# A two-layer graph kernel on one Trainium2 core: the turn to attention in another order, and more of the MLP in the last attention pass

## The chip, the core and the metric

The kernel runs on one core of one Trainium2 chip. The time is device time in microseconds (us); the number quoted for a kernel is the median of several executions. One further execution was recorded by the hardware profiler. Engines are named as in the profile: PE is TensorE (PEld its weight loads), DVE is VectorE, ACT is ScalarE, POOL is GpSimd, SP is SyncE, which here only issues DMAs.

## What is computed

The graph has 3327 nodes of 1024 features, and an adjacency matrix of which about 1% is set. The two layers, cut to what matters:

```python
# layer 0
h  = relu(layernorm(x))
s  = quant4(relu(quant4(h) @ quant3(norm(weight)) * deltas))
x  = x + adj @ s * deltas
# layer 1: attention with 8 heads of 64, then an MLP
h  = relu(layernorm(x))
Wh = einsum('nf,hfd->hnd', h, W)
e  = leaky_relu(e_src[:, :, None] + e_dst[:, None, :], 0.2)   # Wh.a1, Wh.a2
att = softmax(where(adj > 0, e, -9e15), axis=-1)
enc = elu(att @ Wh), heads side by side                       # 3327 x 512
out = relu(enc @ W1.T + b1); out = relu(out @ W2.T + b2); out = relu(out @ W3.T + b3)
x   = x + out @ W4.T + b4
```

## The kernel before

**Layer 0.** The nodes are 26 tiles of 128 rows. For each row tile t, PE sums adjacency times support over all 26 column tiles in fp32r, with each adjacency block as a high and a low half (L717). Adjacency pieces `at` of up to 7 blocks are loaded by SP (L186); ACT makes `hi` (L190), DVE makes `lo` (L194) and one mask byte per edge (L195), which POOL stores to `mask_d` (L201). The result is emptied by ACT into `y` (L732, called `emptied` in the code), scaled by DVE (L733, `resumed`), added to `x` (L734), stored by POOL (L735), and normalised on DVE and ACT up to the factor `r` (L738, `lacking`).

**Heads.** y must be transposed for the product with the head weights. For tiles 0 to 24 this is done by DMA (`transposed_by_dma`): ACT splits y into halves of words (L612), SP issues two transposing DMAs (L614; the second is `turned`), and ACT joins the halves to `ht` (L617). For the last tile PE transposes (`transposed_by_tensor`: two batches of four, L632, each copied from PSUM by ACT, L636). `heads` then runs 8 fp32 matmuls, which the trace shows as 16 records (`whm`, L646), empties them on ACT (`wht`, L653, `taken`), and works out the source and destination scores (L660, L661), their exponentials (L666, L686: ACT loads an exp table for them) and the feature rows (L687 to L697), which POOL stores.

**Attention** is 32 passes: 8 heads by 4 sets of destination tiles (7, 6, 7 and 6 of them, `SUBS`). A pass walks through 13 pairs of source tiles in 7 groups (`GROUPS`; six of two pairs, and pair 6 alone). `select` makes the selectors for a group, two groups ahead of their use: for each source tile a comparison `over` of a row of scores, `srow`, with that tile's scores (ACT, L839; pair 6 on DVE, L833), then per pair an AND with the mask (L846) and an XOR (L847) on DVE. `sums` multiplies selectors with features (L866): 7 tiles x 8 matmuls in a group, into 7 PSUM banks. `closing` finishes a pass (L885 to L914) in slices between the next pass's groups.

**The turn** from layer 0 is written out by hand. On PE the order is: last layer-0 tile, whm of tile 24, sums of group 0, first and second transposes of tile 25, sums of group 1, whm of tile 25, sums of group 2. `queue_behind(a, b)` puts a behind b on their engine without a semaphore; `pin` keeps an instruction in program order on its engine; `issue_after` holds a DMA back until another instruction has run. All adjacency masks come back from `mask_d` through SP (L792), as do the score rows (L801) and features (L786). The scores of groups 0 and 1 (8 pieces of `over`) are ordered ahead of `emptied`.

**The end.** In the last pass `first_layer` runs the first MLP layer of the first group of four node tiles between the groups of sums (L1022, ReLU L1030), through one PSUM bank (`m_ps`). After the pass come that group's second and third layer (L1096, ReLU L1106), and then for each pair of tiles seven products that make up the fourth layer (L1164), from sums of blocks of weights (`weight_sums`, L1066) and of activations (`combined`), with the next group's layers in gaps between them. `joined` loads and joins (L1117) the attention output of a group. Buffers: `over` has 2, `sel` 6, `m_ps` 1, `yo` (output rows) 3.

Of the kernel before, what the change touches and what calls it, by code (L numbers as in the profile page):

```python
# [8 lines left out]
F32 = mybir.dt.float32  # L9
BF16 = mybir.dt.bfloat16  # L10
F32R = mybir.dt.float32r
U8 = mybir.dt.uint8
# [10 lines left out]
P = 128  # L23
# [4 lines left out]
F = 1024  # L28
# [38 lines left out]
def two_layer_kernel(  # L67
# [105 lines left out]
    with tc.tile_pool(name="at", bufs=2, reuse_waits="tile") as atp:  # L173
# [419 lines left out]
        with tc.tile_pool(name="wh", bufs=1, reuse_waits="tile") as whp, tc.tile_pool(  # L593
# [10 lines left out]

            def transposed_by_dma(y):


                ht = s2.tile([P, KF, P], F32, name="ht", bufs=1)
                parts = []
                for c in range(FC):  # L610
# [3 lines left out]
                    last = nc.sync.dma_start_transpose(yht, yh.rearrange("p two f -> p (two f)"))  # L614
                    parts.append(yht)
                for c, yht in enumerate(parts):
                    nc.scalar.copy(  # L617
                        halves_of_words(
                            ht[:, c * KF // FC : (c + 1) * KF // FC].rearrange("p k i -> p (k i)")
                        ),  # L620
                        yht.rearrange("p (two k) i -> p two (k i)", two=2),
                    )
                return ht, last
# [130 lines left out]
            of_k, products, *_, taken = heads(*before, own=f_even)  # L754
            queue_behind(products[0], lacking)
            queue_behind(taken, lacking)
            ht, turns, copies = transposed_by_tensor(y)
            last_of_k, *_ = heads(T - 1, ht, r, own=f_even)
# [6 lines left out]
    with tc.tile_pool(name="over", bufs=2, reuse_waits="tile") as overp, tc.tile_pool(  # L765
        name="srow0", bufs=1, reuse_waits="tile"
    ) as srow0, tc.tile_pool(name="sel", bufs=6, reuse_waits="tile") as selp, tc.tile_pool(
        name="srow1", bufs=1, reuse_waits="tile"
    ) as srow1, tc.tile_pool(name="f1", bufs=1, reuse_waits="tile") as f1p, tc.tile_pool(
# [20 lines left out]
        def load_mask(si, js=slice(0, T)):  # L790
            for b, t in enumerate(SUBS[si]):
                ins = nc.sync.dma_start(masks[si][:, b, js], mask_d[t][:, js])  # L792
            return ins
# [3 lines left out]
        def load_src(i):  # L797
            h, si = attends[i]
            nb = len(SUBS[si])
            srows[i] = (srow1 if i % 2 else srow0).tile([P, 7, P], F32, tag="srow", name="srow")[:, :nb]  # L800
            return nc.sync.dma_start(  # L801
                srows[i].rearrange("p b i -> p (b i)"), src_d[si][h].partition_broadcast(P)
            )
# [17 lines left out]
        def select(n):  # L821
            ends = {}
            i, g = steps[n]
            h, si = attends[i]
            nb = len(SUBS[si])
            mask = masks[si].bitcast(U32)
            for pair in GROUPS[g]:
                over = overp.tile([P, 7, 2, P], U8, tag="over", name="over")[:, :nb]
                for q in range(2):
                    j = 2 * pair + q  # L830
                    if pair in BY_VECTOR:
                        pin(
                            nc.vector.tensor_scalar(  # L833
                                over[:, :, q], srows[i], ndst[:, j, h : h + 1], 255.0, ALU.is_gt, ALU.mult
                            )
                        )
                    else:
                        ends["scalar"] = pin(
                            nc.scalar.activation(  # L839
                                over[:, :, q], srows[i], AF.Relu, bias=large_dst[:, j, h : h + 1], scale=BIG  # L840
                            )
                        )
                sel = selp.tile([P, 2, 7, 2, P], U8, tag="sel", name="sel")
# [95 lines left out]
        select(0)  # L939
        ends = select(1)  # L940
        queue_behind(emptied, ends["scalar"])
        queue_behind(resumed, ends["vector"])
        turn = [(of_k[-1], turns[0][0]), (turns[-1][1], last_of_k[0]), (last_of_k[-1], None)]
        closed = None
        first_group = iter(())
        for n, (i, g) in enumerate(steps):
            if n + AHEAD < len(steps):
                select(n + AHEAD)
# [6 lines left out]
            if (i, g) == (len(attends) - 1, 0):  # L955
# [4 lines left out]
                def nodes(name):  # L960
# [8 lines left out]
                rest = large(mlp, "rest", [P, 7 * NP // 4])  # L969
                bb4 = rest[:, :F]  # L970
                bb1, bb2, bb3 = (rest[:, F + 4 * q : F + 4 * q + 4] for q in range(3))
                h1_0 = rest[:, F + 16 : F + 16 + D1 // P * 512].rearrange("p (m c) -> p m c", c=512)
                enct0 = rest[:, 2 * F + 16 : 2 * F + 16 + EMB // P * 512].rearrange(
                    "p (k c) -> p k c", c=512
# [34 lines left out]
                nc.sync.dma_start(bb4, b4.partition_broadcast(P))  # L1009

                def first_layer():

                    for k in range(EMB // P):

                        nc.scalar.copy(
                            halves_of_words(enct0[:, k]), by_feature(enc_x1[0][0], 512)[:, :, k]
                        )
                        yield
                    for m in range(D1 // P):
                        ps = m_ps.tile([P, 512], F32, tag="mps", name="h0_ps")  # L1020
                        for k in range(EMB // P):
                            nc.tensor.matmul(  # L1022
                                ps,
                                w1[:, k, m * P : (m + 1) * P],
                                enct0[:, k],
                                start=(k == 0),
                                stop=(k == EMB // P - 1),
                            )
                            if k == EMB // P - 1:
                                nc.scalar.activation(  # L1030
                                    h1_0[:, m], ps, AF.Relu, bias=bb1[:, m : m + 1]
                                )
                            yield

                first_group = first_layer()
# [14 lines left out]
        w4c = [[w4[:, 2 * k : 2 * k + 2, c * 512 : (c + 1) * 512] for c in range(FC)] for k in range(2)]  # L1050
        t2, t3, t4 = (
            masks[3].rearrange("p b j i -> p (b j i)").bitcast(F32)[:, n * F : (n + 1) * F].rearrange(
                "p (k c) -> p k c", k=2
            )
            for n in range(3)
        )
        t1 = w4c[0][1]

        def weight_sums():
            for d, one, other in (  # L1060
                (t3, w4c[1][1], w4c[0][1]),
                (t1, w4c[0][1], w4c[0][0]),
                (t2, w4c[1][1], t1),
                (t4, w4c[1][0], t2),
            ):
                pin(nc.vector.tensor_tensor(d, one, other, ALU.subtract))  # L1066
                yield

        of_weight = weight_sums()
        next(of_weight)  # L1070
        next(closed)
        next(of_weight)
        next(of_weight)
        for _ in closed:
            pass
        next(of_weight)


    with tc.tile_pool(name="s4", bufs=2, reuse_waits="tile") as s4, tc.tile_pool(
# [3 lines left out]
        enc_x1.append(nodes("nodes1"))  # L1083
# [169 lines left out]
```

## Time and profile before

| What | Value |
|---|---|
| Median of three runs | 2150.71 us (2149.31 to 2151.26) |
| The profiled execution | 2151.75 us |
| Its span in the trace | 2150.0 us |
| Mean granted PE clock | 0.994 |
| Layer 0 ends on PE (last L717) | 905.66 us |
| Sums of group 2 begin | 943.91 us |
| Last sums of attention end | 1872.97 us |
| Third MLP layer begins (L1096) | 1885.29 us |

The span lies inside the profiled execution's own time. Times within the trace count from the span's start. In a profile row, `x` gives the number of instructions, a number in brackets at the end is idle time of the engine just before the row and what ended it, and PEclk is the share of the full clock that PE was granted.

### The profile page before, as it was taken

Reading aid. Unit: us, or ns where it says so; the run is one execution under the profiler, and the core shown is the slowest. Engines: PE = TensorE matmul, PEld = TensorE weight load, DVE = VectorE, ACT = ScalarE, POOL = GpSimd, SP = SyncE. Lnnn points to the kernel's source line nnn. Section 1 sums busy time; section 2 is a strip of 40 time slices with the busy share of each in tenths; the row PEclk is TensorE's granted clock in tenths of the full one; section 3 lists DMA queues with packets and bytes.
Section 4 is the critical chain, followed back from the end, with each engine's and each line's share of the span. In section 5 each row is a group of like instructions: output and inputs, shape, how many; then the busy total and the mean of one; then the engine's idle time right before and its main releaser. Section 6 shows DMA issues by size and latency. Waiting matters only on the chain.

```text
span 2150.0 us, 36618 instructions
## 1 busy us (share of the span) xinstructions
PE 2101.4 (98%) x15099; PEld 1693.6 (79%) x15109; DVE 1406.8 (65%) x2564; ACT 1347.6 (63%) x1752; POOL 155.8 (7%) x243
## 2 busy tenths in 40 slices
PE   5999999999999999989999999999999999999999
PEld 2467777777777777779999999999999999744444
DVE  8845556555655566467777777777777777635446
ACT  6734454445544554668888888888888888542321
POOL 2300000000100000100000000000000000000000
PEclk9999999999999999989999999999999999999999
DMA  6654544455445544771202021120212114453322
GB/s 217 173 167 137 160 153 136 140 168 153 131 142 165 155 134 147 215 264 26 74 17 74 22 53 46 25 73 19 70 25 74 26 30 126 102 126 108 102 94 74
DMA packets 184648, 233.22 MB, mean 108 GB/s; under 512 B 103924, under 2 KB 133060, under 8 KB 184480
## 3 DMA queue, kind: packets, MB, share of 16 engines
q1 hardware_dynamic: 169692, 178.40, 27.8%
q0 software_dynamic: 14720, 52.41, 7.9%
q8 instruction: 118, 1.93, 0.4%
q14 instruction: 50, 0.41, 0.1%
q10 hardware_dynamic: 68, 0.06, 0.0%
HBM read 141.21 MB, written 66.02 MB: 96 GB/s over the span
## 4 chain that ended last, share of the span: by engine, by line
PE 56%; DVE 1%; ACT 0%; issue 0%; DVEq 0%; ACTq 0%
PE acc L866 43%; PE o L1164 7%; PE h_ps L1096 5%; PE h_ps L1022 0%; PE whm L646 0%; ACT enct L1117 0%; DVE su L885 0%; DVE mask L1066 0%; DVE over L833 0%; DVE su L890 0%; DVE prod L660 0%; DVE ft L687 0%; DVE ft L692 0%; DVE weights L1066 0%; DVE stats L146 0%
## 5 line engine op out<-in xcount | busy, mean ns | idle before, releaser
L866 PEld LDWEIGHTS <-sel 128*128 128x128 fp8e4 x10816 | 935.1, 98 | 9.8 <-issue 8.3
L839 ACT ACTIVATE over<-srow,large_dst 128x896 uint8<-128x896 f32 (+1 forms) x768 | 685.9, 975 | 31.7 <-DVE sel L846 31.7
L866 PE MATMUL acc<-f_even,sel 128*128 128x195 bf16 x5408 | 470.8, 249 | 5.6 <-ACT wht L653 5.6
L866 PE MATMUL acc<-f_odd,sel 128*128 128x195 bf16 x5408 | 467.2, 248 | 0.0
L717 PE MATMUL mm<-s_int,hi 128*128 128x512 f32 x1352 | 426.3, 396 | 0.0
L717 PE MATMUL mm<-s_int,lo 128*128 128x512 f32 x1352 | 416.8, 390 | 0.0
L846 DVE TENSOR_TENSOR sel<-over,mask 128x448 uint32<-128x448 uint32 (+1 forms) x416 | 244.0, 587 | 210.3 <-ACT over L839 123.1
L717 PEld LDWEIGHTS mm<-s_int,hi 128*128 128x128 f32 x1352 | 254.0, 188 | 62.4 <-issue 11.5
L717 PEld LDWEIGHTS mm<-s_int,lo 128*128 128x128 f32 x1352 | 253.8, 188 | 52.7
L847 DVE TENSOR_TENSOR sel<-sel,mask 128x448 uint32<-128x448 uint32 (+1 forms) x416 | 246.0, 591 | 14.2
L190 ACT CAST hi<-at 128x896 fp32r<-128x896 f32 x104 | 92.4, 889 | 153.7 <-PE mm L717 73.4
L646 PE MATMUL whm<-whead,ht 128*128 128x512 f32 x416 | 182.7, 592 | 0.0
L195 DVE TENSOR_SCALAR mk<-at 128x896 uint8<-128x896 f32 (+1 forms) x104 | 59.3, 590 | 173.5 <-DMA at<-in_adj_t 173.5
L194 DVE TENSOR_TENSOR lo<-at,hi 128x896 fp32r<-128x896 f32 x104 | 106.2, 1021 | 68.3 <-ACT hi L190 68.1
L646 PEld LDWEIGHTS whm<-whead,ht 128*128 128x128 f32 x416 | 78.9, 190 | 89.0 <-issue 86.8
L885 DVE TENSOR_REDUCE su<-acc 128x130 f32<-128x390 f32 x208 | 115.8, 556 | 12.2 <-PE acc L866 12.2
L914 POOL DMA_DIRECT2D enc_d<-eh x64 | 57.5, 903 | 856.8 <-ACT eh L912 827.7
L899 ACT ACTIVATE ht<-su,rs 128x64 f32<-128x64 f32 x208 | 53.1, 335 | 104.8 <-DVE rs L895 104.8
L1106 ACT ACTIVATE h<-h_ps,rest 128x512 f32<-128x512 f32 (+1 forms) x54 | 35.3, 655 | 126.3 <-PE h_ps L1096 126.3
L342 PE MATMUL mm<-w_int,xqt 128*128 128x512 bf16 x406 | 93.5, 384 | 7.1 <-DVE w_int L473 4.5
L653 ACT ACTIVATE wht<-whm,lnr 128x512 f32<-128x512 f32 x26 | 17.8, 686 | 121.3 <-PE whm L646 116.4
L617 ACT COPY ht<-yht 128x1024 uint16<-128x1024 uint16 x50 | 67.5, 1355 | 34.0 <-DMA yht<-yh 34.0
(184 smaller groups left out, 1696.0 us busy)
## 6 DMA issues: line engine op xcount, KB each, us to landing
at<-in_adj_t SPq DMA_DIRECT2D x52, 448.0 KB, 4.7
feat_d<-fw POOLq DMA_DIRECT2D x26, 780.0 KB, 6.4
at<-in_adj_t SPq DMA_DIRECT2D x52, 384.0 KB, 4.1
x_d<-xt POOLq DMA_DIRECT2D x26, 512.0 KB, 2.9
nodes<-x_d SPq DMA_DIRECT2D x26, 512.0 KB, 5.5
xt<-in_x SPq DMA_DIRECT2D x25, 512.0 KB, 4.0
out<-yo SPq DMA_DIRECT2D x50, 256.0 KB, 2.2
xs<-in_x SPq DMA_DIRECT2D x24, 512.0 KB, 4.4
```

The costliest lines, as they stand in the source:

```text
L190: ins = nc.scalar.copy(hi, at)
L194: nc.vector.tensor_tensor(lo, at, hi.bitcast(F32), ALU.subtract)
L342: nc.tensor.matmul(mms[t][:, r], xqts[t][:, k, :], w_int[:, k, r], start=(k == 0), stop=(k == KF - 1))
L646: ins = nc.tensor.matmul(whm, ht[:, k, :], whead[:, k, :], start=(k == 0), stop=(k == KF - 1))
L717: nc.tensor.matmul(mm[:, c * 512 : (c + 1) * 512], which[:, q, :], s_int[j][:, c * 512 : (c + 1) * 512], start=(j == 0 and which is hi), s ...
L839: nc.scalar.activation(over[:, :, q], srows[i], AF.Relu, bias=large_dst[:, j, h : h + 1], scale=BIG)
L846: pin(nc.vector.tensor_tensor(up, over.bitcast(U32), of_pair, ALU.bitwise_and))
L847: ends["vector"] = pin(nc.vector.tensor_tensor(dn, up, of_pair, ALU.bitwise_xor))
L866: ins = nc.tensor.matmul(accs[i, b][:, r], chosen[i, pair][:, s, b, q], f[:, j, r], start=(j == 0 and s == 0), stop=(j == T - 1 and s == 1),)
L885: nc.vector.tensor_reduce(su[:, b], accs.pop((i, b)).rearrange("p (q s c) -> p q c s", q=2, s=3), AX.X, ALU.add)
L1096: ins = nc.tensor.matmul(pss[m][:, :cols], wt[:, k, m * P : (m + 1) * P], xt[:, k, :cols], start=(k == 0), stop=(k == k_n - 1),)
L1164: nc.tensor.matmul(ps, st[:, k, q // 2], mv[:, k], start=(k == 0), stop=(k == 1))
```

## The change

Five things are changed.

1. Both halves of mask 0 (14 DMAs) are issued on POOL's queue and without a wait for anything on SP.
2. The pools of the two score rows change places in the order of allocation, so that `srow0` takes another address, and the load of the first row stands on SP ahead of both transposes of tile 24.
3. On ACT, the scores of group 0 stand first, then both joins of tile 24, then `emptied`; the scores of group 1 follow. `copies[0]` (the first PSUM copy of tile 25) is ordered behind `taken` of tile 24, the first exponential of tile 24 (`ratio`, L666) behind the second copy, and the scores of group 2 behind `taken`.
4. `over` is laid out as 2 x (7 x 128) bytes in place of 7 x 2 x 128; the AND reads it through a rearranged view.
5. The end: buffers for a second group are allocated in the last pass, and that group's first loads are issued there. In that pass group 0's joins stand at group 1, the first and second layer's matmuls at groups 2 to 6 (3, 3, 2, 2 and 2 matmuls), and the weight sums and the second group's joins at group 5. After the pass: third layer of group 0, first layer of group 1, then the products. The loads and joins of later groups are issued after the first pair's products.

```diff
-            of_k, products, *_, taken = heads(*before, own=f_even)
+            of_k, products, _, powers, _, taken = heads(*before, own=f_even)
             queue_behind(products[0], lacking)
             queue_behind(taken, lacking)
             ht, turns, copies = transposed_by_tensor(y)
+            queue_behind(copies[0], taken)
+            queue_behind(powers[0], copies[-1])
...
-        name="srow0", bufs=1, reuse_waits="tile"
-    ) as srow0, tc.tile_pool(name="sel", bufs=6, reuse_waits="tile") as selp, tc.tile_pool(
         name="srow1", bufs=1, reuse_waits="tile"
-    ) as srow1, ...
+    ) as srow1, tc.tile_pool(name="srow0", bufs=1, reuse_waits="tile") as srow0, tc.tile_pool(
+        name="sel", bufs=6, reuse_waits="tile"
...
-                over = overp.tile([P, 7, 2, P], U8, tag="over", name="over")[:, :nb]
+                over = overp.tile([P, 2, 7 * P], U8, tag="over", name="over")[:, :, : nb * P]
...
-                                over[:, :, q], srows[i], AF.Relu, bias=large_dst[:, j, h : h + 1], scale=BIG
+                                over[:, q], srows[i], AF.Relu, bias=large_dst[:, j, h : h + 1], scale=BIG
...
+                over = over.bitcast(U32).rearrange("p q (b i) -> p b q i", b=nb)
-                pin(nc.vector.tensor_tensor(up, over.bitcast(U32), of_pair, ALU.bitwise_and))
+                pin(nc.vector.tensor_tensor(up, over, of_pair, ALU.bitwise_and))
...
-        ins = load_mask(0, slice(0, TH))
-        with tc.issue_after(ins.ins):
-            ins = load_src(0)
-        queue_behind(turned, ins)
+        for js in (slice(0, TH), slice(TH, T)):
+            load_mask(0, js, nc.gpsimd)
+        queue_behind(planes[0], load_src(0))
         with tc.issue_after(turned.ins):
-            load_features(0, range(7))
-            ins = load_mask(0, slice(TH, T))
+            ins = load_features(0, range(7))
...
-        select(0)
-        ends = select(1)
-        queue_behind(emptied, ends["scalar"])
+        ends = select(0)
+        queue_behind(joins[0], ends["scalar"])
+        queue_behind(joins[1], joins[0])
+        queue_behind(emptied, joins[1])
         queue_behind(resumed, ends["vector"])
+        select(1)
...
-                select(n + AHEAD)
+                ends = select(n + AHEAD)
+                if n == 0:
+                    queue_behind(ends["first"], taken)
...
+                def layer(yt, xt, wt, bt):
+                    for m in range(yt.shape[1]):
                         ps = m_ps.tile([P, 512], F32, tag="mps", name="h0_ps")
+                        for k in range(xt.shape[1]):
+                            pin(nc.tensor.matmul(ps, wt[:, k, m * P : (m + 1) * P], xt[:, k], ...))
+                            if k == xt.shape[1] - 1:
+                                pin(nc.scalar.activation(yt[:, m], ps, AF.Relu, bias=bt[:, m : m + 1]))
                             yield
+                def early_layers():
+                    yield from layer(h1_0, enct0, w1, bb1)
+                    yield from layer(h2_0, h1_0, w2, bb2)
...
+            if i == len(attends) - 1:
+                if g == 1:
+                    join(enct0, enc_x1[0][0])
+                for _ in range((0, 0, 3, 3, 2, 2, 2)[g]):
+                    next(first_group)
             first, last = sums(n)
...
-            if i == len(attends) - 1:
-                for _ in range(2):
-                    next(first_group, None)
...
+            if (i, g) == (len(attends) - 1, 5):
+                weight_sums()
+                join(joined_1, enc_x1[1][0])
...
-        encs = {1: joined(1)}
-        h = dense(h1_0, w2, bb2, len(groups[0]) * P, "h2", by_input=True)
-        h3 = dense(h, w3, bb3, len(groups[0]) * P, "h3", by_input=True)
+        h3 = dense(h2_0, w3, bb3, len(groups[0]) * P, "h3")
+        encs = {1: joined_1}
...
-                if g + 2 < len(groups):
-                    encs[g + 2] = joined(g + 2)
...
-            of = combined(h3, len(tiles) // 2)
+            if g == 0:
+                next_layer()
+            of = combined(h3, len(tiles) // 2)
-            at = [(0, 6), (1, 2), (1, 5)] if g == 0 else [(0, 2), (0, 6), (1, 2)]
+            at = [(0, 6), (1, 2)] if g == 0 else [(0, 2), (0, 6), (1, 2)]
...
+                if pair == 0 and g + 2 < len(groups):
+                    encs[g + 2] = joined(g + 2)
```

More of the change, by code (lines that the diff above doesn't have):

```diff
@@ L603, in two_layer_kernel @@
             a2_t = whp.tile([P, EMB], F32, name="a2_t")
+            joins, planes = [], []
             def transposed_by_dma(y):
@@ L609, in transposed_by_dma @@
                 parts = []
+                joins.clear()
+                planes.clear()
                 for c in range(FC):
@@ L613, in transposed_by_dma @@
                     yht = s2.tile([P, KF, P], U16, name="yht", bufs=2)
-                    last = nc.sync.dma_start_transpose(yht, yh.rearrange("p two f -> p (two f)"))
+                    planes.append(nc.sync.dma_start_transpose(yht, yh.rearrange("p two f -> p (two f)")))
                     parts.append(yht)
                 for c, yht in enumerate(parts):
[L617 to L621, printed above, removed]
+                    joins.append(
+                        nc.scalar.copy(
+                            halves_of_words(
+                                ht[:, c * KF // FC : (c + 1) * KF // FC].rearrange("p k i -> p (k i)")
+                            ),
+                            yht.rearrange("p (two k) i -> p two (k i)", two=2),
+                        )
                     )
-                return ht, last
+                return ht, planes[-1]
             def transposed_by_tensor(y):
@@ L765, in two_layer_kernel @@
     with tc.tile_pool(name="over", bufs=2, reuse_waits="tile") as overp, tc.tile_pool(
-        name="srow0", bufs=1, reuse_waits="tile"
-    ) as srow0, tc.tile_pool(name="sel", bufs=6, reuse_waits="tile") as selp, tc.tile_pool(
         name="srow1", bufs=1, reuse_waits="tile"
-    ) as srow1, tc.tile_pool(name="f1", bufs=1, reuse_waits="tile") as f1p, tc.tile_pool(
+    ) as srow1, tc.tile_pool(name="srow0", bufs=1, reuse_waits="tile") as srow0, tc.tile_pool(
+        name="sel", bufs=6, reuse_waits="tile"
+    ) as selp, tc.tile_pool(name="f1", bufs=1, reuse_waits="tile") as f1p, tc.tile_pool(
         name="s3", bufs=1, reuse_waits="tile"
@@ L788, in load_features, with load_mask @@
             )
-        def load_mask(si, js=slice(0, T)):
+        def load_mask(si, js=slice(0, T), queue=nc.sync):
             for b, t in enumerate(SUBS[si]):
-                ins = nc.sync.dma_start(masks[si][:, b, js], mask_d[t][:, js])
+                ins = queue.dma_start(masks[si][:, b, js], mask_d[t][:, js])
             return ins
@@ L799, in load_src @@
             nb = len(SUBS[si])
[L800 to L803, printed above, removed]
+            srows[i] = (srow1 if i % 2 else srow0).tile([P, 7 * P], F32, tag="srow", name="srow")[:, : nb * P]
+            return nc.sync.dma_start(srows[i], src_d[si][h].partition_broadcast(P))
         def last_src():
@@ L833, in select @@
                             nc.vector.tensor_scalar(
-                                over[:, :, q], srows[i], ndst[:, j, h : h + 1], 255.0, ALU.is_gt, ALU.mult
+                                over[:, q], srows[i], ndst[:, j, h : h + 1], 255.0, ALU.is_gt, ALU.mult
                             )
@@ L839, in select @@
                             nc.scalar.activation(
-                                over[:, :, q], srows[i], AF.Relu, bias=large_dst[:, j, h : h + 1], scale=BIG
+                                over[:, q], srows[i], AF.Relu, bias=large_dst[:, j, h : h + 1], scale=BIG
                             )
                         )
+                        ends.setdefault("first", ends["scalar"])
                 sel = selp.tile([P, 2, 7, 2, P], U8, tag="sel", name="sel")
@@ L969, in two_layer_kernel @@
                 rest = large(mlp, "rest", [P, 7 * NP // 4])
+                enc_x1.append(nodes("nodes1"))
+                joined_1 = large(mlp, "joined_1", [P, EMB // P, 512])
                 bb4 = rest[:, :F]
                 bb1, bb2, bb3 = (rest[:, F + 4 * q : F + 4 * q + 4] for q in range(3))
-                h1_0 = rest[:, F + 16 : F + 16 + D1 // P * 512].rearrange("p (m c) -> p m c", c=512)
-                enct0 = rest[:, 2 * F + 16 : 2 * F + 16 + EMB // P * 512].rearrange(
-                    "p (k c) -> p k c", c=512
+                h1_0, h2_0, enct0 = (
+                    rest[:, F + 16 + 512 * at : F + 16 + 512 * (at + n)].rearrange("p (m c) -> p m c", c=512)
+                    for at, n in ((0, D1 // P), (D1 // P, D2 // P), ((D1 + D2) // P, EMB // P))
                 )
@@ L1009, in two_layer_kernel, with join @@
                 nc.sync.dma_start(bb4, b4.partition_broadcast(P))
-                def first_layer():
+                load_encoded(1, range(4, 8))
+                def join(xt, enc):
                     for k in range(EMB // P):
[L1015 to L1019, printed above, removed]
-                        ps = m_ps.tile([P, 512], F32, tag="mps", name="h0_ps")
[L1021 to L1027, printed above, removed]
-                            )
[L1029 to L1032, printed above, removed]
+                        pin(nc.scalar.copy(halves_of_words(xt[:, k]), by_feature(enc, 512)[:, :, k]))
@@ new lines, in layer @@
+                def layer(yt, xt, wt, bt):
+                    for m in range(yt.shape[1]):
+                        ps = m_ps.tile([P, 512], F32, tag="mps", name="h0_ps")
+                        for k in range(xt.shape[1]):
+                            pin(
+                                nc.tensor.matmul(
+                                    ps,
+                                    wt[:, k, m * P : (m + 1) * P],
+                                    xt[:, k],
+                                    start=(k == 0),
+                                    stop=(k == xt.shape[1] - 1),
+                                )
+                            )
+                            if k == xt.shape[1] - 1:
+                                pin(nc.scalar.activation(yt[:, m], ps, AF.Relu, bias=bt[:, m : m + 1]))
@@ L1033, in first_layer @@
                             yield
-                first_group = first_layer()
+                def early_layers():
+                    yield from layer(h1_0, enct0, w1, bb1)
+                    yield from layer(h2_0, h1_0, w2, bb2)
+                w4c = [[w4[:, 2 * k : 2 * k + 2, c * 512 : (c + 1) * 512] for c in range(FC)] for k in range(2)]
+                t2, t3, t4 = (
+                    masks[3].rearrange("p b j i -> p (b j i)").bitcast(F32)[:, n * F : (n + 1) * F].rearrange(
+                        "p (k c) -> p k c", k=2
+                    )
+                    for n in range(3)
+                )
@@ new lines, in two_layer_kernel, with weight_sums @@
+                t1 = w4c[0][1]
+                def weight_sums():
+                    for d, one, other in (
+                        (t3, w4c[1][1], w4c[0][1]),
+                        (t1, w4c[0][1], w4c[0][0]),
+                        (t2, w4c[1][1], t1),
+                        (t4, w4c[1][0], t2),
+                    ):
+                        pin(nc.vector.tensor_tensor(d, one, other, ALU.subtract))
+                first_group = early_layers()
+            if i == len(attends) - 1:
[3 more added lines that the diff above has]
+                    next(first_group)
@@ L1045, in two_layer_kernel @@
                 next(closed, None)
-            if i == len(attends) - 1:
-                for _ in range(2):
-                    next(first_group, None)
[L1050 to L1073, printed above, removed]
+            if (i, g) == (len(attends) - 1, 5):
+                weight_sums()
+                join(joined_1, enc_x1[1][0])
         for _ in closed:
             pass
-        next(of_weight)
     with tc.tile_pool(name="s4", bufs=2, reuse_waits="tile") as s4, tc.tile_pool(
@@ L1081, in two_layer_kernel @@
     ) as ps_p, tc.tile_pool(name="s4_o", bufs=4, space=PSUM, reuse_waits="tile") as o_ps:
-        enc_x1.append(nodes("nodes1"))
         groups = [range(t0, min(t0 + 4, T)) for t0 in range(0, T, 4)]
```

## The prediction

> **What bounds the kernel now.** I read the busy rows first, then TensorE's waits, then time windows around each wait.
>
> ```profile
> PE 2101.4 (98%) x15099; PEld 1693.6 (79%) x15109; DVE 1406.8 (65%) x2564; ACT 1347.6 (63%) x1752; POOL 155.8 (7%) x243
> ```
>
> TensorE (PE) is busy 98% of the span, and the change takes no matmul away. So time can come only from PE's idle time and from stretches where its clock is low. The view of waits, for PE:
>
> ```profile
> PE h_ps L1096 <- ACT h L1106: 8.0, 1, 8.0
> ...
> PE acc L866 <- ACT wht L653: 5.6, 1, 5.6
> ...
> PE tp L632 <- ACT ht L636: 3.7, 1, 3.7
> ```
>
> The lines left out lie in the first 60 us, which the change does not touch. The three shown (17.3 us) stand at the two places it rewrites: the turn from layer 0 to attention (905 to 944 us) and the step from attention to the MLP (1873 to 1894). Between them the windows view shows attention itself with no gap:
>
> ```profile
> core 0: us, PE busy (x) PEld busy (x) DVE busy (x) ACT busy (x) POOL busy (x), PEclk, DMA share, GB/s
> 915.00:920.00 5.00, 0.00 (x0) 0.00 (x0) 5.00 (x12) 2.75 (x5) 0.08 (x1) 0.73 1.04 402
> 922.00:924.00 2.00, 2.00 (x15) 1.83 (x13) 1.89 (x6) 0.49 (x3) 0.00 (x0) 0.50 1.03 399
> 926.00:929.00 3.00, 0.00 (x0) 0.00 (x0) 2.56 (x4) 1.69 (x3) 0.00 (x0) 0.76 1.04 405
> 931.00:933.00 2.00, 2.00 (x15) 1.85 (x13) 0.06 (x1) 2.00 (x4) 0.73 (x1) 0.50 1.03 399
> 935.00:937.00 2.00, 2.00 (x26) 2.00 (x24) 0.00 (x0) 0.00 (x0) 0.00 (x0) 1.00 1.06 389
> ...
> 1887.00:1889.00 2.00, 2.00 (x4) 0.81 (x3) 0.00 (x0) 2.00 (x3) 0.00 (x0) 0.50 1.20 267
> ...
> 944.00:1851.00 907.00, 907.00 (x10530) 906.99 (x10529) 692.18 (x1342) 771.42 (x1047) 56.67 (x64) 1.00 0.21 56
> ```
>
> PE's clock is 0.50 behind each wait: 13 to 15 attention matmuls in 2 us instead of 26 at 1.00. Finer windows put 0.50 at 917.36 to 924.18, 927.58 to 934.41 and 1879.90 to 1890.15. Cold work lies in 920.56 to 924.18, 929.29 to 934.41 and 1885.29 to 1890.15; half of each is lost: 1.8, 2.55 and 2.4 us. **So the turn loses 5.57 + 1.8 + 3.69 + 2.55 = 13.6 us and the end 0.75 (h2's 8 records: 4.19 us instead of 8 x 0.43, with a wait on DVE su) + 7.99 + 2.4 = 11.1.**
>
> What sets the turn shows in ACT's timeline:
>
> ```profile
> 910.78 1.09 ACT L732 ACTIVATE y<-mm,r_asf 128x1024 f32<-128x1024 f32 x1
> 911.78 3.83 ACT L839 ACTIVATE over<-srow,large_dst 128x896 uint8<-128x896 f32 x4
> 917.86 0.20 ACT L136 ACTIVATE lns<-lnv 128x1 f32<-128x1 f32 x1 [2.25 <-DVE lnv L151]
> 917.97 1.96 ACT L839 ACTIVATE over<-srow,large_dst 128x896 uint8<-128x896 f32 x2
> 919.84 0.67 ACT L653 ACTIVATE wht<-whm,lnr 128x512 f32<-128x512 f32 x1
> ```
>
> PE ends layer 0 (mm(25)) at 905.66, but y, its evacuation, waits for seven scores (`over`, 0.96 us each) and starts 5.1 us late. LayerNorm follows y on DVE, and wht(24) is ordered behind both. wht(24) frees the bank of the fourth accumulator, so PE stops after 24 of 56 matmuls.
>
> **The turn, step by step.** SP's queue before:
>
> ```profile
> 887.94 5.08 SPq L792 DMA_DIRECT2D mask<-mask_d  x7
> 893.12 2.80 SPq L614 DMA_TRANSPOSE yht<-yh  x1
> 896.02 0.53 SPq L801 DMA_DIRECT2D srow<-src_d  x1
> 896.63 3.25 SPq L614 DMA_TRANSPOSE yht<-yh  x1
> ```
>
> (1) *Mask 0 to POOL.* SP loses 5.08 and later 4.02 us of issue; POOL gains 14 DMAs of 208 KB. Nearest rows are POOL's own issues of 128-row transfers, 0.540 us (L735) and 0.563 (L201), so 14 x 0.55 = 7.7 us on an engine busy 7%. They start when the mask area is free, as before, and seven need about 4 us of issue and 6 of flight: about 899, before DVE's first AND. Behind them on POOL are only x1_d's store and the feature stores. [...] L735's 26 issues lie beside a DVE that works throughout, yet span 537 to 554 ns; I take the row.
>
> (2) *Scores load.* After the pools swap, srow0 lies over the last adjacency piece. The load waits for DVE's `lo` of that piece (896.67), 0.6 us later than now, and both transposes of tile 24 are ordered behind it on SP: 3.6 us later for the first (893.12), 0.7 for the second. Unloaded transposes land in 3.0 to 3.1 us (here 7.7 and 6.3 behind seven masks), so at about 902 and 904. A srow lands in 3.4: about 901.
>
> (3) *ACT order* is now four scores, two joins, y, four scores, then wht. Scores 901 to 904.9 (3.83), joins (L617) to 907.5 at 1.35 each. whm(24) needs the first join at 906.3: PE waits 0.4 to 0.6 that it doesn't now. y runs 907.6 to 908.7, 3.1 earlier; the LayerNorm chain to L738 took 920.9 - 911.9 = 9.0 with two ANDs and a DVE score inside, now some 6 to 6.5: wht at about 915.2. PE ends whm and 24 matmuls at 915.4. **The 5.57 and its 1.8 go (0.2 may stay).**
>
> (4) sums(0) ends at 918.2, tp's first four transposes at 918.8. But its copy on ACT is ordered behind wht and the next scores: four scores 3.83, table load 1.28, two exps, from 915.9 on: about 922. **PE idles about 3.5 us here, as now.** Warm, the order behind (1.1 half-warm transposes, 56 matmuls 4.83, whm 6.9) reaches sums(2) at 934.75, cold at 937, against 943.91. Gain 9.2 or 7.0.
>
> [...] But the trace has a 3.69 us stretch (925.60 to 929.29) whose clock was halved at 927.58[...], and cost 2.55. I take the row[...].
>
> **Attention.** `over` is written contiguously (0.958 and 0.85 us a piece now, in runs of 128 bytes) and the AND reads it in runs of 128 bytes. PE's 907.00 of 907.00 hides any gain. AND is 0.621 us; DVE does about 25 us of each 31.4 us pass of seven tiles, so its 13 ANDs may each grow 6.4 / 13 = 0.49 before PE waits. Bounds: -0.1 to +0.62 each; I take 0, as both forms move equal bytes.
>
> **The end.** Joins of group 0 (4.88 us on ACT) move to the last pass's second group; first- and second-layer matmuls (12 in all, two records of 0.43 each; the last 4 lay after the pass) to groups 2 to 6; weight sums (4.8 us DVE) and joins of group 1 to group 5, where ACT has 11 us free. Two transposing loads of group 1 go with them, onto SP behind the weights, in a pass where the DMA share is a fifth:
>
> ```profile
> 1869.18 0.69 ACT L1030 ACTIVATE rest<-h_ps,rest 128x512 f32<-128x512 f32 x1 [11.05 <-PE h_ps L1022]
> ...
> 1885.29 9.52 PE L1096 MATMUL h_ps<-h,weights 128*128 128x512 f32 x16 [7.99 <-ACT h L1106]
> ```
>
> The third layer then only needs h2 and starts where the pass ends: all 11.1 go. Group 1's first layer runs on joins done by about 1876; it moves ahead of the products, so `combined` on DVE gets 6.9 us more cover. Later groups' transposing loads are now issued behind a pair's products and ahead of the next output stores on SP: stores leave some us later, and three `yo` buffers cover that.
>
> **A new wait takes some back.** The early layers share one PSUM bank (m_ps). The first product of output m1 stands in group 3 on PE, about 1855.4; the bank is freed by m0's ReLU, pinned on ACT behind joins and the scores of groups 3 and 4: joins 1845.7 to 1850.6, four scores to 1854.0, eh 0.85, four scores to 1858.2, ReLU to 1858.9. **PE waits 3.5 us**; before, that ReLU came at 1857.44 with no wait behind it. If that wait halves the clock, 2 more. Net end: 11.1 - 3.5 - 0.2 (joins late for group 2) = 7.4 warm; 5.5 taken, with that wait cold.
>
> **Sum.** Turn 7.0 + end 5.5 = 12.5 us with cold residues; 9.2 + 7.4 = 16.6 warm. The profiled execution took 2151.75 (span 2150.0): 2139.2. It ran 1.04 above the median 2150.71, so I forecast 2138.2.
>
> **Rivals.**
> - *Residues warm* [...]: -16.6, 2134.1. [...] Against: the 3.69 row.
> - *Scores first delays the layer:* srow or transposes are late because feature loads and POOL's masks fill the DMA engines (share 1.04 to 1.11 in these windows). Each microsecond past 901 goes straight onto whm(24), y and wht; 3 to 5 us gives 2141 to 2143.
> - *The end gains nothing,* since ACT's added 10 us in the last pass also delay PE's scores: the turn's 7.0 alone gives 2143.7, less up to 5 us of such waits 2149. Against: PE-bound passes, and ACT's 11 free.
> - *Slower:* AND's new read pattern doubles it to 1.24 us. 13 x 0.62 = 8.1 us on a 25 us pass makes DVE the bound at 33.1 against 31.4: 1.7 x 16 passes = 27, minus 12.5: 2165. It decides from 0.49 us a piece. Against: equal bytes and runs of 128 bytes.
> - *Order not obeyed:* ACT's program order has joins ahead of y and wht behind the scores, so no.
>
> **How the numbers follow.** Forecast .55, warm .15, late scores .17, end without gain .08, slower .05. A measurement of this kernel can tell 0.2% (4.3 us) from no change: only the end case and the slower one reach above 2146.4. Faster .88, same .07, slower .05. Range 2132.5 to 2144.5: warm to late scores.
>
> **What would show it.** Right: PE's wait on wht gone; PE waits of about 3.5 us on ACT ht (tp) and on ACT's ReLU (early layer); the 8.0 wait gone; POOL's masks near 0.55 us; AND still 0.62 and 0.55. Wrong: POOL issues of microseconds, whm(24) starting after 907.5, a wait of PE on DVE sel inside attention, or PE held by scores in the last pass.

## The result and the profile after

The changed kernel takes 2143.76 us (median of seven, 2142.01 to 2146.50) against 2150.89 for the kernel before on the same chips: a ratio of 0.9967, with an interval of 0.9956 to 0.9979. That is 7.1 us faster, where 12.5 were forecast. The profiled execution took 2143.69 us, its span is 2141.8; the traces of before and after lie 8.2 us apart, since the profiled execution of before ran 1 us above its median.

The busy row of the page, and PE's waits in the order of their cost (engine, line, what ended the wait, us in total, times, longest; the lines left out lie in the first 60 us):

```profile
PE 2099.7 (98%) x15099; PEld 1690.6 (79%) x15109; DVE 1392.0 (65%) x2564; ACT 1346.9 (63%) x1752; POOL 163.6 (8%) x257
```

```profile
PE whm L652 <- ACT ht L622: 6.4, 1, 6.4
...
PE h_ps L1034 <- ACT rest L1043: 2.9, 1, 2.9
PE tp L638 <- ACT ht L642: 2.2, 1, 2.2
```

The three waits that the change aimed at (8.0, 5.6 and 3.7) have become these. The 8.0 is gone, for a 2.9 that was forecast as 3.5. The 5.6 is gone too, but a wait of 6.4 us stands one step earlier, in front of whm(24), where 0.4 to 0.6 was forecast. The 3.7 is now 2.2. PE and ACT in the turn show it (start, duration, engine and line, the bracket is the idle time before):

```profile
911.91 10.05 PE L652 MATMUL whm<-whead,ht 128*128 128x512 f32 x16 [6.37 <-ACT ht L622]
921.79 5.00 PE L874 MATMUL acc<-f_even,sel 128*128 128x195 bf16 x56
926.63 0.60 PE L638 MATMUL tp<-ident,y 128*128 128x128 f32 x4
929.48 0.66 PE L638 MATMUL tp<-ident,y 128*128 128x128 f32 x4 [2.25 <-ACT ht L642]
```

```profile
901.40 3.85 ACT L845 ACTIVATE over<-srow,large_dst 128x896 uint8<-128x896 f32 x4 [6.23 <-DMA srow<-src_d]
910.53 2.52 ACT L622 COPY ht<-yht 128x1024 uint16<-128x1024 uint16 x2 [5.28 <-DMA yht<-yh]
912.91 1.10 ACT L738 ACTIVATE y<-mm,r_asf 128x1024 f32<-128x1024 f32 x1
```

The scores run where the prediction had them (901.4 to 905.2, forecast 901 to 904.9). Then ACT waits 5.28 us, not for an engine but for the transposing DMAs of tile 24. The first of them was issued at 896.57 and landed 13.9 us later; PE stands still from 905.54 and then runs whm(24) partly at half clock (PEclk 0.50 from 908 to 916), 10.05 us for what takes 7.05.

In all, from the end of layer 0 on PE to the sums of group 2 the turn took 36.16 us in place of 38.25. With 0.1 from an earlier layer 0 that is 2.2 us gained, where 7.0 were forecast. Attention is untouched: from there to the end of the last pass's group 2, with the six records of early layers that now stand in between (2.60 us) left out, 907.79 us against 907.78. From there to the end of the span, with those six records counted in, are 292.31 us against 298.31: 6.0 gained, forecast 5.5. The last pass, on PE:

```profile
1852.09 1.05 PE L1034 MATMUL h_ps<-rest,weights 128*128 128x512 f32 x2
1856.07 3.42 PE L1034 MATMUL h_ps<-rest,weights 128*128 128x512 f32 x4 [2.94 <-ACT rest L1043]
1859.28 2.52 PE L874 MATMUL acc<-f_odd,sel 128*128 128x195 bf16 x24
...
1879.25 7.05 PE L1108 MATMUL h_ps<-rest,weights 128*128 128x512 f32 x16
```

The third layer follows the last sums with no gap. In front of it stands the new wait on the one PSUM bank: 2.94 us, and then four records in 3.42 us where 1.91 is usual, at half clock (PEclk 0.50 from 1858.0 to 1859.5).

Two rows answer questions that the prediction left open: POOL's issues of masks (count, busy us and mean ns), and the AND with its new read pattern.

```profile
L800 POOL DMA_DIRECT2D mask<-mask_d x14 | 7.8, 567 | 2.9 <-DMA feat_d<-fw 2.9
```

```profile
L854 DVE TENSOR_TENSOR sel<-over,mask 128x448 uint32<-128x448 uint32 x208 | 128.9, 620 | 91.7 <-ACT over L845 64.9 <-PE acc L874 24.2 <-PE mm L723 0.9
L854 DVE TENSOR_TENSOR sel<-over,mask 128x384 uint32<-128x384 uint32 x208 | 114.8, 552 | 132.2 <-PE acc L874 72.2 <-ACT over L845 56.3 <-DMA srow<-src_d 2.0
```

The AND takes 620 and 552 ns (621 and 553 before): no cost, and the slower rival falls. POOL's issues take 0.567 us (the longest 0.914), not microseconds.

So the question is why the transposes took 13.9 us. Two causes were at hand. **Contention:** POOL's second seven masks were issued at 896.03 to 899.74, beside the transposes, on another queue. **Queue:** the change put the score row in front of the transposes on SP and let both leave at once. The issues of the two transposes and of POOL's second seven masks, and the time from issue to landing of the transposes:

```profile
896.57 6.22 SPq L618 DMA_TRANSPOSE yht<-yh  x2
896.03 3.71 POOL L800 DMA_DIRECT2D mask<-mask_d  x7 [2.90 <-DMA feat_d<-fw]
DMA to landing us min/median/max: 13.9/13.9/13.9
```

### The profile page after: what moved, and what is told of

Same layout as the page of the kernel before. It is cut to its first block, busy times and chain, and to the rows that moved or that the text cites. A ratio compares the mean times of both kernels' runs of the same rounds, so it can differ in the third digit from the quotient of the medians.

```text
span 2141.8 us, 36615 instructions
## 1 busy us (share of the span) xinstructions
PE 2099.7 (98%) x15099; PEld 1690.6 (79%) x15109; DVE 1392.0 (65%) x2564; ACT 1346.9 (63%) x1752; POOL 163.6 (8%) x257
## 4 chain that ended last, share of the span: by engine, by line
PE 94%; DVE 2%; DMA 2%; ACT 2%; issue 0%; SPq 0%; POOL 0%; DVEq 0%; ACTq 0%; POOLq 0%
PE acc L874 42%; PE mm L723 28%; PE whm L652 8%; PE o L1176 7%; PE h_ps L1108 5%; PE mm L342 3%; DMA yht<-yh 1%; ACT over L845 1%; DMA xqt<-xq 0%; DVE stats L255 0%; DMA w<-in_w 0%; PE h_ps L1034 0%; ACT xb L314 0%; DVE w_stats L385 0%; ACT rest L1027 0%
```

## The experiments

The runs were spread over several chips, on which the kernel before took 2150.4 to 2151.4 us. Each ratio is to the kernel before on the same chip; a difference between two experiments is one of medians, and under 1 us it says nothing.

**The second seven masks back on SP, behind the transposes.**

```diff
-        for js in (slice(0, TH), slice(TH, T)):
-            load_mask(0, js, nc.gpsimd)
+        load_mask(0, slice(0, TH), nc.gpsimd)
         queue_behind(planes[0], load_src(0))
         with tc.issue_after(turned.ins):
-            ins = load_features(0, range(7))
+            load_features(0, range(7))
+            ins = load_mask(0, slice(TH, T))
```

> The changed kernel with the second seven masks back on SP, behind the transposes and the first features; nothing else differs. In the changed kernel the two transposes of tile 24 took 13.9 us to land and PE waited 6.4 us for the join behind them. Theory contention (POOL's second seven masks, issued at 896.0 to 899.7, share the DMA engines with the transposes): landing falls to 6 to 8 us, PE's wait on the join to under 1.5, time 5 to 8 us under the changed kernel, about 2136 to 2139. Rival queue (the score row ahead of the transposes on SP, and the two issued at once, are the cause): landing stays at 12 us or more, the wait at 5 or more, time within 1.5 us of the changed kernel's 2143.8.

Measured: 2135.95 us, ratio to before 0.9926 (0.9913 to 0.9938). The transposes landed in 5.7 us and PE waited 1.0:

```profile
DMA to landing us min/median/max: 5.7/5.7/5.7
906.22 7.13 PE L652 MATMUL whm<-whead,ht 128*128 128x512 f32 x16 [0.97 <-ACT ht L622]
913.19 5.00 PE L874 MATMUL acc<-f_even,sel 128*128 128x195 bf16 x56
918.03 0.60 PE L638 MATMUL tp<-ident,y 128*128 128x128 f32 x4
921.70 0.66 PE L638 MATMUL tp<-ident,y 128*128 128x128 f32 x4 [3.07 <-ACT ht L642]
```

Contention holds. With the order of SP unchanged the row in front of the transposes does no harm. Moving 7 of 14 mask loads is worth 7.8 us by the medians, and the turn then comes out as the prediction had it for full clock: tp waits 3.07 us (3.5 forecast) and sums(2) start at 933.91 (934.75; the 937 of half clock was taken).

**The transposes ahead of the score row on SP,** all masks on POOL.

```diff
-        queue_behind(planes[0], load_src(0))
-        with tc.issue_after(turned.ins):
+        ins = load_src(0)
+        queue_behind(ins, turned)
+        with tc.issue_after(ins.ins):
             ins = load_features(0, range(7))
```

> The changed kernel with both transposes of tile 24 ahead of the first score row on SP, the masks all on POOL as in the change. Theory queue: transposes issued at about 893.1 and 894.6 as their halves come, land in 3 to 6 us; PE's wait on the join then comes only from the scores, which stand ahead of the joins on ACT: the row lands at about 901 to 903, so 2 us of wait and 2140. Theory contention: landing stays above 9 us since the fourteen masks and the feature store fill the engines until 900 whatever the order; transposes come in at 903 to 906, the row at 904 to 908, PE waits 4 to 8 us and the time is 2142 to 2146.

Measured: 2154.68 us, ratio 1.0013 (1.0007 to 1.0020), slower than before. Both theories had it faster than that (2140, and 2142 to 2146), but the direction speaks for contention: issued as early as 891.7, the transposes took 19.2 us, to 910.9. What stands behind them on SP suffers too, and more. The row was issued at 900.16 and ACT got it at 918.69; the joins follow the scores, so most of PE's wait of 18.5 us is the row's:

```profile
918.69 3.84 ACT L845 ACTIVATE over<-srow,large_dst 128x896 uint8<-128x896 f32 x4 [23.78 <-DMA srow<-src_d]
922.44 2.50 ACT L622 COPY ht<-yht 128x1024 uint16<-128x1024 uint16 x2
```

**Only the end of the change,** on the kernel before (its diff is the last part of the change's).

> The kernel before with only the end of the change (second layer, weight sums and joins in the last pass); the turn as before. If the parts add up, the traces give 6.3 us to the end: 2144.5, with PE's wait of about 2.9 us on the early layer's ReLU and the waits of 5.6 and 3.7 in the turn still there. Rival [...]: less than 4 or more than 9 us gained.

Measured: 2145.85 us, ratio 0.9970 (0.9959 to 0.9982). The parts add up within what can be measured, and the old turn shows its waits of 5.9 and 2.8. It gains 5.6 us, so the end is worth what the prediction gave it (5.5).

**Early layers spread 4, 2, 2, 2, 2 over the groups.**

```diff
-                for _ in range((0, 0, 3, 3, 2, 2, 2)[g]):
+                for _ in range((0, 0, 4, 2, 2, 2, 2)[g]):
```

> The changed kernel with the early layers' matmuls spread 4, 2, 2, 2, 2 over groups 2 to 6 in place of 3, 3, 2, 2, 2, so that the first output's ReLU frees the PSUM bank a group earlier. Theory (the one bank costs 2.9 us of wait and about 2 more at half clock): 4.5 to 5 us faster than the changed kernel, 2139, with no PE wait on ReLU over 0.5. Rival (the wait only covers late scores of groups 4 and 5): PE waits on DVE sel instead and gains under 2 us.

Measured: 2139.89 us, ratio 0.9941 (0.9927 to 0.9954), 3.9 under the changed kernel. The wait on the ReLU is gone and none has taken its place. Its turn was 0.8 us later than the changed kernel's (sums(2) at 942.54), so the repair itself is worth the 4.7 that the rows give: 2.94 + (3.42 - 1.91) + (2.52 - 2.23).

**The second seven masks later on POOL, by order alone,** in two forms; the diff is the first, and the second names ACT's first join (`joins[0]`) in place of `turned`.

```diff
-        for js in (slice(0, TH), slice(TH, T)):
-            load_mask(0, js, nc.gpsimd)
+        load_mask(0, slice(0, TH), nc.gpsimd)
...
         with tc.issue_after(turned.ins):
+            load_mask(0, slice(TH, T), nc.gpsimd)
```

> The changed kernel with the second seven masks still on POOL's queue, but held back until the second transpose has been issued on SP; the previous run put them on SP, behind the transposes in the same queue. Theory order of the queue (what protects the transposes is that the masks stand behind them in one queue): on the other queue they still compete, landing stays over 11 us and the time is within 2 us of the changed kernel's 2143.8. Rival head start (it is enough that the transposes are issued first): landing 6 to 7 us and 2136 to 2138, like the run with the masks on SP.

> The changed kernel with the second seven masks still on POOL's queue, but only after the first join of tile 24, so that both transposes have landed. Theory overlap (only what runs beside the transposes on another queue hurts them): transposes land in 5 to 6 us, PE's wait on the join is under 1.5 us, 2135 to 2138, like the run with these masks on SP. Rival (POOL's queue is slow for these masks in any place): the masks of the later source tiles come too late for the ANDs of groups 3 and 4 behind the feature loads, PE waits on DVE sel there and the time is over 2139.

Measured: 2145.12 us and 2144.03, ratios 0.9972 (0.9960 to 0.9983) and 0.9965 (0.9953 to 0.9978). Neither tests anything. Across two queues `issue_after` put in no wait here (to say that it holds a DMA back until another instruction has run is too much): the traces have these masks leaving POOL from 896.4 and 896.8, as in the change, though `turned` was issued at 897.6 in the first and the first join ran at 909.6 in the second. They are two repeats of the changed kernel: landing 13.0 and 12.6 us, waits of 5.4 and 5.0.

**The same with a real wait:** the first of the second seven waits by semaphore for ACT's first join.

```diff
+        for b, t in enumerate(SUBS[0]):
+            ins = nc.gpsimd.dma_start(masks[0][:, b, TH:], mask_d[t][:, TH:])
+            if b == 0:
+                tc.add_manual_dep(ins.ins, joins[0].ins.name, DependencyInfo(Sync, DATA), ...)
...
```

> The changed kernel with the second seven masks on POOL's queue, the first of them now with a real wait for ACT's first join of tile 24. (In the two runs that held these masks back by order alone, the order of POOL's queue did not change and the masks left at 896.4 and 896.8 as in the change, so they tested nothing.) Theory overlap (what runs beside the transposes on the other queue hurts them): the masks leave after about 904, transposes land in 5 to 6 us, PE's wait on the join is under 1.5 us, 2135 to 2138. Rival (POOL's queue is a bad place for these masks at any time): PE waits on DVE sel in the groups that need them, over 2139.

Measured: 2137.09 us, ratio 0.9936 (0.9922 to 0.9950). The masks left at 907.23, the transposes landed in 4.6 us, PE waited for no join and for no selector. POOL's queue is no bad place for these masks; beside the transposes is:

```profile
DMA to landing us min/median/max: 4.6/4.6/4.6
907.23 3.89 POOL L933 DMA_DIRECT2D mask<-mask_d  x7 [12.66 <-ACT ht L622]
```

**Three of the seven on POOL, four on SP.**

> The second seven masks split: three on POOL at the old place, four on SP behind the transposes. If the delay goes with the bytes beside the transposes, landing is near 5.7 + 3/7 of (13.9 - 5.7) = 9.2 us, PE waits about 3 us and the time is about 2139. Rival (any transfer left on the other queue is enough): landing over 12 and 2142 or more.

Measured: 2138.09 us, ratio 0.9943 (0.9930 to 0.9955); landing 10.2 us, wait 2.6. The delay grows with what runs beside the transposes: 4.5 to 5.7 us with none of the seven (five kernels), 10.2 with three (one), 12.6 to 14.4 with seven (four).

**All of mask 0 on SP, as before, the rest as in the change.**

```diff
-        for js in (slice(0, TH), slice(TH, T)):
-            load_mask(0, js, nc.gpsimd)
+        queue_behind(planes[0], load_mask(0, slice(0, TH)))
         queue_behind(planes[0], load_src(0))
         with tc.issue_after(turned.ins):
-            ins = load_features(0, range(7))
+            load_features(0, range(7))
+            ins = load_mask(0, slice(TH, T))
```

> The changed kernel with the whole of mask 0 on SP as before (first half ahead of the score row, second half behind the transposes); scores first, pools, layout and end as in the change. Theory (the first half has landed before the transposes need the engines, so the queue it came by doesn't matter): within 1.5 us of the run with only the second half on SP, 2135 to 2137.5. Rival (POOL's early start of the first half is what lets the row and the transposes through): transposes land 2 us or more later, 2138 to 2141.

Measured: 2136.98 us, ratio 0.9931 (0.9919 to 0.9944), landing 4.5 us. The first half is as good on SP: nothing in the change needs POOL's queue for masks. This is the change without its first part, and it gains 13.9 us.

**Only the masks on POOL,** on the kernel before.

> The kernel before with only the first part of the change: all of mask 0 on POOL, nothing else. Theory: the transposes, which before landed in 6.3 and 7.7 us behind seven masks, now compete with fourteen on another queue and take over 11; they come in at 904 to 907 and PE waits for the join before tile 24's heads; the turn's two old waits stay. Slower than before by 1 to 5 us: 2152 to 2156. Rival (with the old order of ACT the join had some 2 us of slack, and SP's freed 9 us of issue bring the features and later loads sooner): within 1 us of before or faster, 2146 to 2152.

Measured: 2159.81 us, ratio 1.0036 (1.0023 to 1.0050): by the medians 8.4 us slower than before, more than expected. The joins come at 902.63 and 912.56, so PE stops in the middle of whm(24) for 4.3 us, and since ACT's scores follow the joins here, the old wait on wht grows from 5.6 to 7.8:

```profile
PE acc L866 <- ACT wht L653: 7.8, 1, 7.8
PE whm L646 <- ACT ht L617: 4.3, 1, 4.3
```

**The two repairs together, and a third.** The first run below has the second seven masks on SP and the 4, 2, 2, 2, 2 spread. The second also lets ACT take the first copy of the last tile's transposes ahead of tile 24's exponentials and of the scores of group 4:

```diff
             queue_behind(copies[0], taken)
+            queue_behind(powers[1], copies[0])
+            queue_behind(powers[2], copies[0])
...
                 if n == 0:
                     queue_behind(ends["first"], taken)
+                if n == 2:
+                    queue_behind(ends["first"], copies[0])
```

> Second seven masks on SP and early layers 4, 2, 2, 2, 2 together. If the two gains add (7.8 and 3.9 us under the changed kernel): 2132. Rival, they share something: above 2134.

> As the run with both repairs, and on ACT the first copy of the transposed last tile stands ahead of the exponentials (with their table load) of tile 24 and of the scores of group 4. Theory: PE's wait of 3.1 us on that copy falls to about 0.6, 2.4 us faster than without, 2129.5 to 2130. Rival: the selectors of group 1 on DVE are late next, since they follow LayerNorm there, and the wait moves to DVE sel with under 1 us gained.

Measured: 2133.02 us (0.9913, 0.9899 to 0.9926), so the gains add up (2132 if they did so fully), and 2130.92 (0.9903, 0.9889 to 0.9916). This last kernel is 20.0 us faster than the kernel before on the same chip, and 12.8 faster than the changed one by the medians. Its turn on PE:

```profile
906.39 7.13 PE L652 MATMUL whm<-whead,ht 128*128 128x512 f32 x16
913.36 5.00 PE L876 MATMUL acc<-f_even,sel 128*128 128x195 bf16 x56
918.20 0.60 PE L638 MATMUL tp<-ident,y 128*128 128x128 f32 x4
919.47 0.66 PE L638 MATMUL tp<-ident,y 128*128 128x128 f32 x4 [0.68 <-ACT ht L642]
919.97 4.99 PE L876 MATMUL acc<-f_even,sel 128*128 128x195 bf16 x56
924.80 7.05 PE L652 MATMUL whm<-whead,ht 128*128 128x512 f32 x16
```

Sums(2) start at 931.69, 25.3 us after layer 0's end, against 38.25 before; every group of matmuls runs at full clock (7.13, 5.00, 4.99 and 7.05 us, where the changed kernel's whm(24) took 10.05).

## Why the prediction was right or wrong

It was right that the kernel would be faster, and the time lies in its range near the upper end; the gain is 7.1 us of the 12.5. The runs, each against its own kernel before, split it: the end alone gains 5.6, all of the change but the masks' move 13.9, so the rest of the turn 8.3 (7.0 forecast), and the move of the masks, put at nothing, costs 6.8. That term is what failed: step (1) priced the masks as issues only, and step (2) took the transposes beside them as unloaded. That the range holds the measured time is owed to the room it left for late scores.

*The turn: wrong, in step (2).* The step put the transposes' landing at about 902 and 904, from 3.0 to 3.1 us "unloaded". (Its own terms, issue at 896.7 and 897.3 and 3.1 us each, give about 900; nothing hangs on that, as the joins stand behind the scores until 904.9.) They were not unloaded: step (1) of the same sum had just put seven more masks on POOL, leaving beside them. The join came at 910.53 in place of 904.9. PE waited 6.37 us for 0.5, and whm(24) lost 3.0 to the half clock behind that wait: 8.9 us against the sum. Some came back later: tp waited 2.25 us and stayed at full clock, where 3.5 and 2.2 were put down (3.4). That leaves some 5.5 lost, near the 4.8 between forecast and measured gain of the turn. With the seven masks out of the way the step came true (whm(24) forecast for 906.3, seen at 906.22; wht for 915.2, seen at 914.23), though the transposes still took 5.7 us and not 3.1. Of the prediction's signs of being wrong, one came: whm(24) after 907.5, at 911.91.

*The rival that happened.* "Scores first delays the layer" named POOL's masks filling the DMA engines as its reason and gave 2141 to 2143, at a chance of .17. Of its reason, the masks are what the runs show; no run takes the feature loads away. The order of ACT that it is named after is innocent; with the masks back on SP the same order gives 2136.98. One other account came closer in number, by luck: "the end gains nothing" (2143.7), where the end gained all that was forecast.

*Step (1).* The row was right on the price of an issue (0.567 us, 0.55 taken), and no mask issue took over 0.914 us. The row's issues lay beside a busy DVE (for all of their 14.0 us); of the masks' that holds only in part, as DVE was busy for 1.91 of the 4.12 us of the first seven and for 0.13 of the 3.71 of the second. But issue time was not all that the step cost: with all the rest of the change in place, the move to POOL costs 6.8 us (2143.76 against 2136.98), and alone it costs 8.4. Its DMAs were counted as issues on POOL and not as traffic beside SP's.

*The end: right, and the terms near.* All of the old loss went. The new wait on the bank was found ahead and measures 2.94 us, with 1.8 us of half clock behind it (3.5 and 2 forecast). The end gained 6.0 (5.5).

*Attention: right.* It took the value nothing between bounds of -0.1 and +0.62 per AND; measured is -0.001 us.

*Warm or cold (full or half clock).* For the idle stretch at tp the prediction took half clock, from the row of before (3.69 us of idle time); that the clock would stay full was its other estimate. In the changed kernel the stretch was 2.25 us and stayed warm, so the 2.2 us put down for half clock there were not lost. Where the stretch was some 3.07 us, near the 3.5 forecast, the clock was halved in three kernels and full in one (5.91 to 6.19 us for the 56 sums behind, and 5.00), so the pick was open to luck; more of it stands below.

## What to carry to other kernels

Moving transfers to another engine's queue takes away their issue time, and also the order that kept them behind something urgent: ask of each what will now run beside it, above all beside transposing DMAs that a busy engine waits for (landed in 13.9 us here, and in 5.7 with the masks behind them). (Only POOL's queue was tried here; whether a third engine's would do the same is open.) A duration from a quiet stretch may be put into a sum only if the same sum leaves that stretch quiet (the transposes: 3.1 us in the quiet, 13.9 with seven masks beside them). Before a small product is slotted between large ones, see which instruction frees its one PSUM bank and what is pinned ahead of that (2.94 us of wait here, none with the 4, 2, 2, 2, 2 spread).

## What the runs showed of the hardware that was not expected

**Transposes and mask loads on two queues slow each other far beyond their bytes.** DMA traffic by queue (packets, MB, share of 16 engines' time), for the changed kernel from 902 to 904 us, its slowest two:

```profile
q0 software_dynamic: 32, 0.12, 77.5%
q1 hardware_dynamic: 77, 0.02, 19.3%
```

and for the kernel with the second seven masks on SP, from 900 to 902, with the transposes all but alone:

```profile
q1 hardware_dynamic: 1434, 0.37, 90.3%
```

Both queues together moved 0.14 MB in 2 us with the engines counted as 97% taken, where the transposes moved 0.37. In the 13.9 us from the issue of the transposes the changed kernel moved 2.96 MB, the other in as long 4.23. The masks suffer too: the seven took 11.4 us to land (median) beside the transposes on POOL, and 5.7 behind them on SP. What makes 32 packets take so long was not tried and stays open.

**The clock can halve after an idle stretch of 2.25 us, and need not.** In the changed kernel PE idled 2.25 us at tp and kept the full clock (5.00 us for the 56 sums behind). In the run with three masks on POOL the idle stretch was 2.25 us as well, and the clock was halved some 0.7 us after work had resumed at 925.34 (6.61 us for the same sums; in the run with the transposes first as well):

```profile
922.00:925.00 3.00, 1.09 (x12) 0.85 (x9) 2.97 (x8) 2.97 (x6) 0.00 (x0) 1.00 1.02 393
925.00:926.00 1.00, 0.66 (x6) 0.65 (x7) 1.00 (x2) 1.00 (x2) 0.00 (x0) 1.00 1.07 409
926.00:926.50 0.50, 0.50 (x6) 0.47 (x5) 0.41 (x2) 0.50 (x2) 0.00 (x0) 0.57 0.92 359
927.00:929.00 2.00, 2.00 (x14) 1.83 (x13) 2.00 (x3) 2.00 (x5) 0.00 (x0) 0.50 1.03 403
```

The columns are the window, its length, busy us of PE, PEld, DVE, ACT and POOL, the granted clock, DMA share and GB/s. Two runs with an idle stretch of 3.07 us each differ in the same way: full clock with the second masks on SP (its rows stand above), half clock in the same kernel with the early layers spread:

```profile
921.48 1.11 PE L638 MATMUL tp<-ident,y 128*128 128x128 f32 x4 [3.07 <-ACT ht L642]
922.39 6.10 PE L874 MATMUL acc<-f_even,sel 128*128 128x195 bf16 x56
```

So at 2.25 us, and again at 3.07, the length alone did not decide; what did is not shown. In the kernel before the clock fell 2.4, 2.0 and 2.6 us after PE had stopped (at 914.98, 925.60 and 1877.30; halved from 917.36, 927.58 and 1879.90).

**A comparison on DVE gained from the new layout of `over`, unseen in the time.** Before and after, the rows of pair 6's scores:

```profile
L833 DVE TENSOR_SCALAR over<-srow,ndst 128x896 uint8<-128x896 f32 x32 | 35.2, 1137 | 0.0
L839 DVE TENSOR_SCALAR over<-srow,ndst 128x896 uint8<-128x896 f32 x32 | 20.5, 680 | 0.0
```

Seven tiles took 1137 ns and now take 680; six took 614 and take 611, and ACT's scores of seven tiles took 1028 ns and still do. That is nearly all of why DVE is busy for 1392.0 us in place of 1406.8. The run with only the masks on POOL, on the old layout, has 1138 ns, the one with the second masks on SP 681. Attention is bound by PE (busy for 903.64 of the 903.64 us from 941.70 to 1845.34), so it buys no time here. The row of scores is now also handed over in another shape, and which of the two did it was not tried.
